# Attention sums: 448 accumulating exponentials on ScalarE in place of 512 products with ones on TensorE

## The chip, the cores and the metric

The kernel runs on one core of a Trainium2 chip. The metric is the device time of one execution in microseconds (us), lower is better; the number shown is the median of three runs. One further execution was taken by the hardware profiler, and all lines of the profile come from that one. The engines are named as the profile names them: PE is TensorE's matmuls, PEld its weight loads, DVE is VectorE, ACT is ScalarE, POOL is GpSimd, SP is SyncE.

## The reference

Sixteen sequences of 128 tokens, each token 128 wide, pass through four layers. Each layer adds two gated blocks to `x`: an attention to a context of the same shape, and a feed-forward block. Layers 0, 1 and 3 have mixtures of experts (8, 16 and 32 experts), layer 2 has a block of 64 slots. The change touches the attentions of layers 2 and 3, which have 16 heads of width 8:

```python
# layer 2
scores = jnp.einsum('bhqd,bhkd->bhqk', q, k) * scale
scores = jnp.where(mask == 0, jnp.float32(-1000000000.0), scores)
attn = jax.nn.softmax(scores, axis=-1)
out = jnp.einsum('bhqk,bhkd->bhqd', attn, v)
# layer 3: heads 0-7 at full length, heads 8-15 on every second token
for i, f in enumerate((1, 2)):
    hs = slice(i * HPS, (i + 1) * HPS)
    Qd, Kd, Vd = Q[:, hs, ::f], K[:, hs, ::f], V[:, hs, ::f]
    scores = jnp.einsum('bhqd,bhkd->bhqk', Qd, Kd) * inv_scale
    attn = jax.nn.softmax(scores, axis=-1)
    o = jnp.einsum('bhqk,bhkd->bhqd', attn, Vd)
    outs.append(_upsample_linear(o, S))
```

So for each query and head the kernel needs the largest score, the exponentials of the scores minus it, their sum over the keys, and the values weighted by exponential over sum.

## The kernel before

The sixteen sequences are worked in four groups of four (512 tokens). `experts()` is one long stream of expert steps over the layers 1 and 3 (and part of layer 0), a Python generator; between its steps the main program writes down the attentions of other groups. In the stretch of interest the order in the program is: attention 2 of group g when layer 1's experts of group g are done, attention 3 of group g when the slots of layer 2 for that group are done. The slots and the routing of the next expert block are written down between expert steps. Which instruction an engine runs when is laid down before the launch by the framework's scheduler: it takes what is ready, and what stands earlier in the program goes first. At run time each engine works through its own list in order and waits on semaphores. `in_turn` fixes the order of some matmuls among themselves. `nc.any` leaves it to the scheduler whether a copy runs on VectorE or ScalarE.

An expert step (`gated` and `down`) is two matmuls of 128x512 into the banks `pg` and `pu` (L445, L446), a tanh on ScalarE (L450), two products on VectorE (L451, L457), a product with the routing weight on GpSimd (L461), and, two steps later, the third matmul (L1036). Attentions take their PSUM banks from `ps_mm` (four banks of 512 numbers); the experts, the slots and the routings take theirs from `ps_x` (three banks) and `ps_acc` (one).

An attention tile covers 128 queries of eight or sixteen heads so that its scores fill four banks, four blocks of 128 in each. Attention 2 has four tiles a group, attention 3 two and a half one (the heads on every second token, two halves of 64 rows): 28 tiles in all, 24 full and 4 half. A tile goes so:

- First scores `ps`, queries on the partitions, keys along the row (L588 for the mask and L593 in attention 2, L739 and L772 in attention 3).
- `maxima`: VectorE takes the largest of each block, four instructions (L481), into columns of `mp`.
- `mp` is transposed on TensorE (L599, L745, L778) and added to the spare rows of `qT` (L600, L747, L779), so that the second product comes out with the maximum taken off.
- Second scores `ps`, keys on the partitions, queries along the row (L603 for the mask and L609, L754, L787). They need the same four banks.
- ScalarE takes the exponential of each bank into `pts` (L615, L760, L793), three buffers.
- `weighted` (L483): for each of the four banks four products of the values with `pts` into `po[:, 0, :]` (L487), and four products of `own` with `pts` into `po[:, 1, :]` (L490). `own` holds ones in the eight columns of a head, so the second gives the sum of the exponentials, repeated on the eight rows that hold this head's values. The half tile has eight and eight. `po` lies in a bank of `ps_mm` too (in the half tile in two).
- `over_weights` (L493): VectorE takes the reciprocal of the sums (L495) and multiplies (L496).

A matmul of 4-byte numbers shows as two records in the profile, a transpose as one.

Of the kernel before, what the change touches and what calls it, by code (L numbers as in the profile page):

```python
# [10 lines left out]
F32 = mybir.dt.float32  # L11
# [6 lines left out]
P = 128  # L18
# [8 lines left out]
DK = 8  # L27
# [32 lines left out]
def flamingo(ctx, tc, x_in, ctx_in, mask_in, w1, w2, w3, wslot, wsmall, slots, cols_in, rows_in, consts_in,  # L60
# [371 lines left out]
    def in_turn(chain, ins):  # L432

        if chain:
            tc.add_manual_dep(ins.ins, chain[-1].name,
                              mybir.DependencyInfo(mybir.DependencyClass.NoSync, mybir.DependencyReason.DATA),
                              reason="in_turn")
        chain[:] = [ins.ins]
# [35 lines left out]
    def value(rows, t, h):  # L474

        at = 24 + 32 * h - DK * (h % 4)
        return vp[rows, t, at:at + 32]

    def maxima(mp, i, src, n, k):

        nc.vector.tensor_reduce(mp[:, 0:n, 32 * i + 16:32 * i + 18], src, AX.X, ALU.max)  # L481

    def weighted(chain, heads, r, first, last):  # L483


        for po, jj, vcols, pts, rows in heads:
            in_turn(chain, nc.tensor.matmul(out=po[32 * jj:32 * jj + 32, 0, :], lhsT=vcols, rhs=pts, start=first, stop=last,  # L487
                                     skip_group_check=True))
        for po, jj, vcols, pts, rows in heads:
            in_turn(chain, nc.tensor.matmul(out=po[32 * jj:32 * jj + 32, 1, :], lhsT=own[rows, r, :], rhs=pts, start=False,  # L490
                                     stop=last, skip_group_check=True))

    def over_weights(o, po, n):  # L493
        rc = work.tile([P, P], F32, tag="rcw", name="rcw")
        nc.vector.reciprocal(rc[:, :n], po[:, 1, :])  # L495
        nc.vector.tensor_tensor(o, po[:, 0, :], rc[:, :n], ALU.mult)  # L496


# [69 lines left out]
    def attention_2(g):  # L568
# [15 lines left out]
        for t in range(GB):  # L584
# [5 lines left out]
            for s in range(2):  # L590
                for i in range(4):
                    rr = slice(32 * i, 32 * i + 32)
                    nc.tensor.matmul(out=split(ps[i])[:, 2 * s:2 * s + 2, :], lhsT=qT[rr, s, b], rhs=kTm[rr, s, :, b],  # L593
                                     start=False, stop=True, skip_group_check=True)
            for i in range(4):
                maxima(mp[:, 2 * t:2 * t + 2], i, ps[i][:].rearrange("p (s j k) -> p s j k", s=2, j=2), 2, P)
            pt = tr_tile()
            for s in range(2):
                nc.tensor.transpose(pt[:, s * P:(s + 1) * P], mp[:, 2 * t + s, :], ident[:])  # L599
# [13 lines left out]
            for i in range(4):  # L613
                pts = work.tile([P, 4, P], F32, tag="pts", name="pts", bufs=3)
                nc.scalar.activation(pts[:], split(ps[i]), AF.Exp, scale=scale8)  # L615
                weighted(chain, [(po, jj, value(slice(0, P), t, 4 * jj + i), pts[:, jj, :], slice(0, P)) for jj in range(4)],
                         i, i == 0, i == 3)
            over_weights(oT[:, b], po, P)
        py = split(mm_tile())
        for t in range(GB):  # L620
            mm(py[:, t, :], oT[:, t * P:(t + 1) * P], w(W2, 1))
# [83 lines left out]
    def attention_3(g):  # L705
# [27 lines left out]
        for p in range(2):  # L733
            ps = [mm_tile() for _ in range(4)]
            for u in range(2):
                b = slice((2 * p + u) * P, (2 * p + u + 1) * P)
                for i in range(4):
                    rr = slice(32 * i, 32 * i + 32)
                    nc.tensor.matmul(out=split(ps[i])[:, 2 * u:2 * u + 2, :], lhsT=qa[rr, b], rhs=ka[rr, :, b],  # L739
                                     start=True, stop=True)  # L740
            for i in range(4):
                maxima(mp[:, 2 * p:2 * p + 2], i, ps[i][:].rearrange("p (u j k) -> p u j k", u=2, j=2), 2, P)
            pt = tr_tile()
            for u in range(2):
                nc.tensor.transpose(pt[:, u * P:(u + 1) * P], mp[:, 2 * p + u, :], ident[:])  # L745
# [12 lines left out]
            for i in range(4):  # L758
                pts = work.tile([P, 4, P], F32, tag="pts", name="pts", bufs=3)
                nc.scalar.activation(pts[:], split(ps[i]), AF.Exp, scale=scale8)  # L760
                weighted(chain, [(po, jj, value(slice(0, P), 2 * p + jj // 2, 4 * (jj % 2) + i), pts[:, jj, :], slice(0, P))
                          for jj in range(4)], i, i == 0, i == 3)
            over_weights(oa[:, p, :], po, P)


        ps = [mm_tile()[:, 0:G2].rearrange("p (p2 j k) -> p p2 j k", p2=2, j=2) for _ in range(4)]
# [6 lines left out]
                                     start=True, stop=True)  # L773
        for i in range(4):
            maxima(mp[:, 4:6], i, ps[i], 2, HALF)
        pt = tr_tile()
        for p in range(2):
            nc.tensor.transpose(pt[:, p * P:(p + 1) * P], mp[:, 4 + p, :], ident[:])  # L778
# [12 lines left out]
        for i in range(4):  # L791
            pts = work.tile([P, 4, P], F32, tag="pts", name="pts", bufs=3)
            nc.scalar.activation(pts[:, :, 0:HALF], ps[i], AF.Exp, scale=scale8)  # L793
            halves = [slice(u * HALF, (u + 1) * HALF) for u in range(2)]
            weighted(chain, [(po[u], jj, value(halves[u], jj // 2, 8 + 4 * (jj % 2) + i), pts[halves[u], jj, 0:HALF], halves[u])
                      for jj in range(4) for u in range(2)], i, i == 0, i == 3)
        for u in range(2):
            over_weights(ob[:, u, :], po[u], HALF)


        pz = [mm_tile() for _ in range(2)]
# [352 lines left out]
    W3, W3H = load("w3", w3[:, 2 * D:3 * D]), weights_by_head("w3h", w3)  # L1154

    mp = blank("mp", [P, 8, P])
    own = blank("own", [P, 4, 32])
    for r in range(4):
        nc.gpsimd.memset(own[:, r, DK * r:DK * r + DK], 1.0)


    perm = work.tile([P, 2, P], F32, tag="pts", name="perm", bufs=3)
# [172 lines left out]
```

## Time and profile before

| | |
|---|---|
| median of 3 runs | 928.96 us (928.27 to 929.91) |
| profiled execution | 930.84 us, its span 929.1 us |
| mean granted clock of TensorE | 0.965 |
| busy: PE, PEld | 834.3 us (90%), 468.5 us (50%) |
| busy: DVE, ACT, POOL | 580.6 us (62%), 259.3 us (28%), 282.6 us (30%) |
| instructions: PE, DVE, ACT, POOL | 6183, 1628, 457, 283 |

The span runs from the first to the last instruction; what lies around it is 930.84 - 929.1 = 1.7 us. A busy share is a mean over stages with different limits. The profile's page ends its chain of waits with PE 54%, DVE 21%, POOL 8% and ACT 4% of the span. The costliest groups are GpSimd's products with routing weights (L461, 126 of 1278 ns, 161.0 us) and the three matmuls of the expert steps (L446, L1036 and L445, 288 records each, 154 to 156 us each). Of the attentions: the maxima L481 (65.8 us in 112 instructions), the products with values L487 and with ones L490, the exponentials L615 (64 of 602 ns, 33.6 us), and the reciprocals L495.

In a line of a group stand the line of the kernel, the engine, the operation, output and input with their shapes, the count, the busy time in us and the mean of one in ns, then the idle time of the engine ahead of them and what ended it. In a line of the timeline stand the start in us, the length in us, the engine, the line, the operation and how many were merged; in brackets the idle time before it and what ended that.

### The profile page before, as it was taken

The page shows a single profiled execution, that of the slowest core. Times are in us where ns is not written, and L with a number is a line of the kernel's source. Part 1 is how long each engine was busy: PE and PEld are TensorE (multiplying, and loading weights), DVE is VectorE, ACT ScalarE, POOL GpSimd, SP SyncE. Part 2 cuts the span into 40 slices and gives each one's busy share as a digit, 9 for nine tenths or more (in the row PEclk, how much of TensorE's full clock was granted, in tenths as well). Part 3 has the DMA queues.
Part 4 walks back from the last instruction along what each step waited for, and adds up shares of the span by engine and source line. Part 5 has one row for each costly group of instructions (what it writes and reads, how often), then busy time and mean ns, then how long its engine had stood idle before and what let it go on. Part 6 is the DMA issues. An engine that isn't in the chain of part 4 may idle for free.

```text
span 929.1 us, 16015 instructions
## 1 busy us (share of the span) xinstructions
PE 834.3 (90%) x6183; PEld 468.5 (50%) x6183; DVE 580.6 (62%) x1628; ACT 259.3 (28%) x457; POOL 282.6 (30%) x283
## 2 busy tenths in 40 slices
PE   3889399877999999999899999999989998999997
PEld 3554289534544554455455555555554554554443
DVE  4756252566977475666675866677666668566622
ACT  1222166221321222232223222223222232322321
POOL 3326521353233124311421113421114223313443
PEclk9979699978999999999999999999999999999999
DMA  9711212552121012100202112310002111211231
GB/s 305 211 17 40 64 46 79 159 162 63 24 69 44 27 35 80 46 21 28 69 35 67 35 47 62 123 37 24 24 24 72 35 48 46 76 51 49 94 103 34
DMA packets 55677, 62.12 MB, mean 67 GB/s; under 512 B 14312, under 2 KB 33512, under 8 KB 55472
## 3 DMA queue, kind: packets, MB, share of 16 engines
q1 hardware_dynamic: 53776, 55.90, 19.9%
q0 software_dynamic: 1536, 3.15, 1.1%
q10 hardware_dynamic: 288, 2.03, 0.6%
q8 instruction: 49, 0.80, 0.4%
q14 instruction: 28, 0.23, 0.1%
HBM read 53.97 MB, written 7.09 MB: 66 GB/s over the span
## 4 chain that ended last, share of the span: by engine, by line
PE 54%; DVE 21%; POOL 8%; issue 8%; ACT 4%; DMA 2%; another core or an unknown queue 1%; SPq 1%; POOLq 0%; DVEq 0%; ACTq 0%
PE mm L108 8%; PE acc L1036 7%; PE pg L445 7%; PE pu L446 7%; POOL hw L461 3%; DVE sg L451 3%; PE mm L593 2%; PE po L487 2%; DVE h L457 2%; DVE mp L481 2%; POOL rs L260 2%; POOL y L1017 2%; DVE xn L264 2%; PE tr L244 2%; PE po L490 2%
## 5 line engine op out<-in xcount | busy, mean ns | idle before, releaser
L461 POOL TENSOR_TENSOR hw<-h,cb 128x512 f32<-128x512 f32 x126 | 161.0, 1278 | 459.4 <-DVE h L457 348.1
L446 PE MATMUL pu<-xnTx,wall 128*128 128x512 f32 x288 | 156.4, 626 | 14.9 <-DVE sg L451 13.1
L1036 PE MATMUL acc<-hw,wall 128*128 128x512 f32 x288 | 153.9, 618 | 10.6 <-DVE h L457 9.9
L445 PE MATMUL pg<-xnTx,wall 128*128 128x512 f32 x288 | 154.8, 620 | 7.8 <-issue 4.7
L450 ACT ACTIVATE sg<-pg 128x512 f32<-128x512 f32 x123 | 73.6, 598 | 244.7 <-PE pg L445 230.5
L457 DVE TENSOR_TENSOR h<-sg,pu 128x512 f32<-128x512 f32 x145 | 99.1, 683 | 60.9 <-PE pu L446 40.7
L451 DVE SCALAR_TENSOR_TENSOR sg<-sg,pg 128x512 f32<-128x512 f32 x123 | 83.6, 680 | 51.4 <-ACT sg L450 51.3
L1036 PEld LDWEIGHTS acc<-hw,wall 128*128 128x128 f32 x288 | 55.1, 198 | 71.3 <-issue 53.0
L446 PEld LDWEIGHTS pu<-xnTx,wall 128*128 128x128 f32 x288 | 52.4, 197 | 75.9 <-issue 39.1
L481 DVE TENSOR_REDUCE mp<-mm 128x4 f32<-128x512 f32 (+1 forms) x112 | 65.8, 645 | 21.1 <-PE mm L593 19.9
L445 PEld LDWEIGHTS pg<-xnTx,wall 128*128 128x128 f32 x288 | 50.1, 194 | 50.2 <-issue 35.1
L495 DVE RECIPROCAL rcw<-po 128x128 f32<-128x128 f32 (+1 forms) x28 | 25.2, 900 | 57.1 <-PE po L490 44.8
L264 DVE TENSOR_SCALAR xn<-x,mv,rs 128x128 f32<-128x128 f32 x116 | 40.3, 399 | 25.4 <-POOL rs L260 25.4
L615 ACT ACTIVATE pts<-mm 128x512 f32<-128x512 f32 x64 | 33.6, 602 | 73.3 <-PE mm L609 73.3
L487 PE MATMUL po<-pts,vp 128*32 128x128 f32 (+1 forms) x896 | 46.1, 274 | 7.6 <-ACT pts L615 6.7
L260 POOL TENSOR_TENSOR rs<-ve,neghalf 128x4 f32<-128x4 f32 x32 | 33.2, 1037 | 61.8 <-DVE ve L258 61.7
L490 PE MATMUL po<-pts,own 128*32 128x128 f32 (+1 forms) x896 | 44.3, 266 | 0.5 <-issue 0.5
L453 ACT ACTIVATE sg<-pg 128x512 f32<-128x512 f32 x33 | 19.7, 597 | 67.9 <-PE pg L445 58.4
L487 PEld LDWEIGHTS po<-pts,vp 128*32 128x32 f32 (+1 forms) x896 | 21.3, 108 | 29.9 <-ACT pts L615 14.0
L254 DVE BATCH_NORM_STATS2 st<-x 128x6 f32<-128x128 f32 x128 | 29.5, 280 | 10.2 <-DMA x<-in_x 9.9
L593 PE MATMUL mm<-kTm,qT 32*128 32x256 f32 x256 | 30.5, 413 | 0.0
L1017 POOL DMA_INDIRECT y<-yd,to x24 | 23.7, 987 | 21.7 <-DMA yd<-yb 8.8
(335 smaller groups left out, 1226.0 us busy)
## 6 DMA issues: line engine op xcount, KB each, us to landing
cb<-combD SPq DMA_DIRECT2D x72, 256.0 KB
cb<-combD SPq DMA_DIRECT2D x128, 128.0 KB
wall<-in_gu SPq DMA_DIRECT2D x24, 256.0 KB
wall<-in_dn SPq DMA_DIRECT2D x12, 256.0 KB
xb<-xd SPq DMA_DIRECT2D x7, 256.0 KB
yd<-yb SPq DMA_DIRECT2D x7, 256.0 KB
xd<-vp ACTq DMA_DIRECT2D x1, 1072.0 KB
x<-in_x SPq DMA_DIRECT2D x4, 256.0 KB
```

What stands on the lines that cost most here:

```text
L108: nc.tensor.matmul(out=o, lhsT=l, rhs=r, start=start, stop=stop)
L264: nc.vector.tensor_scalar(xn[:, t, :], x[:, t, :], mv[:, t, 0:1], rs[:, t:t + 1], ALU.subtract, ALU.mult)
L445: in_turn(chain, nc.tensor.matmul(out=pg[:], lhsT=w[:, 0], rhs=xnT[:], start=True, stop=True))
L446: in_turn(chain, nc.tensor.matmul(out=pu[:], lhsT=w[:, 1], rhs=xnT[:], start=True, stop=True))
L450: nc.scalar.activation(sg[:], pg[:], AF.Tanh, scale=0.5)
L451: nc.vector.scalar_tensor_tensor(sg[:], sg[:], 1.0, pg[:], ALU.add, ALU.mult)
L457: nc.vector.tensor_tensor(h[:], sg[:], pu[:], ALU.mult)
L461: (nc.vector if vector else nc.gpsimd).tensor_tensor(hw[:], h[:], cb[:], ALU.mult)
L481: nc.vector.tensor_reduce(mp[:, 0:n, 32 * i + 16:32 * i + 18], src, AX.X, ALU.max)
L487: in_turn(chain, nc.tensor.matmul(out=po[32 * jj:32 * jj + 32, 0, :], lhsT=vcols, rhs=pts, start=first, stop=last, skip_group_check=True))
L490: in_turn(chain, nc.tensor.matmul(out=po[32 * jj:32 * jj + 32, 1, :], lhsT=own[rows, r, :], rhs=pts, start=False, stop=last, skip_group_ch ...
L1036: in_turn(chain, nc.tensor.matmul(out=acc[0][:], lhsT=w[:, 2], rhs=h[:], start=n == 0, stop=last))
```

## The change

The sums are no longer formed by products. A new function `sums_of_weights` follows the maxima of the first scores. For each of the four banks VectorE scales the maxima (`top`), and ScalarE takes the exponential of each block of the first scores in place, with the block's scaled maximum as bias and with the sum over the row as a second output (`accum_out`) into a column of `sums`. VectorE takes the reciprocals of 16 columns, GpSimd spreads each over eight columns (`over`). At the end of the tile `over_sums` turns `over` to the layout of the values by one product with the identity, copies that out of PSUM, and multiplies. The products with `own`, the tile `own` and its five fills go.

```diff
-    def weighted(chain, heads, r, first, last):
+    def sums_of_weights(mp, ps, k):
+        sums = small.tile([P, 16], F32, tag="sums", name="sums")
+        for i in range(4):
+            top = small.tile([P, 2, 2], F32, tag="mxs", name="mxs", bufs=4)
+            nc.vector.tensor_scalar(top[:], mp[:, :, 32 * i + 16:32 * i + 18], -scale8, None, ALU.mult)
+            for a in range(2):
+                for j in range(2):
+                    at = 8 * a + 4 * j + i
+                    nc.scalar.activation(ps[i][:, a, j, :], ps[i][:, a, j, :], AF.Exp, bias=top[:, a, j:j + 1], scale=scale8,
+                                         accum_out=sums[:, at:at + 1])
+        nc.vector.reciprocal(sums[:], sums[:])
+        over = small.tile([P, 16, DK], F32, tag="over", name="over")
+        nc.gpsimd.tensor_copy(over[:], bc(sums[:], 2, DK))
+        return over[:].rearrange("p h d -> p (h d)")
+
+    def weighted(chain, heads, first, last):
...
-        for po, jj, vcols, pts, rows in heads:
-            in_turn(chain, nc.tensor.matmul(out=po[32 * jj:32 * jj + 32, 1, :], lhsT=own[rows, r, :], rhs=pts, start=False,
-                                     stop=last, skip_group_check=True))
-
-    def over_weights(o, po, n):
+    def over_sums(chain, o, po, over, rows):
+        n = o.shape[1]
+        in_turn(chain, nc.tensor.matmul(out=po[:, 1, :], lhsT=over[rows, :], rhs=ident[rows, rows], start=False,
+                                        stop=True, skip_group_check=True))
         rc = work.tile([P, P], F32, tag="rcw", name="rcw")
-        nc.vector.reciprocal(rc[:, :n], po[:, 1, :])
+        nc.any.tensor_copy(rc[:, :n], po[:, 1, :])
         nc.vector.tensor_tensor(o, po[:, 0, :], rc[:, :n], ALU.mult)
...
             for i in range(4):
-                maxima(mp[:, 2 * t:2 * t + 2], i, ps[i][:].rearrange("p (s j k) -> p s j k", s=2, j=2), 2, P)
+                maxima(mp[:, 2 * t:2 * t + 2], i, ps[i], 2, P)
+            over = sums_of_weights(mp[:, 2 * t:2 * t + 2], ps, P)
             pt = tr_tile()
...
-            over_weights(oT[:, b], po, P)
+            over_sums(chain, oT[:, b], po, over, slice(0, P))
...
-    own = blank("own", [P, 4, 32])
-    for r in range(4):
-        nc.gpsimd.memset(own[:, r, DK * r:DK * r + DK], 1.0)
```

The same three edits (the call behind the maxima, the shorter `weighted`, `over_sums` at the end) stand in the full tiles of attention 3 and in its half tile, where `over_sums` is called for each of the two halves.

## The prediction

> **What bounds the kernel now.** I read the forty slices of the span first, then the attention stretches by window, then one attention tile in order of time, then the groups by line and shape.
>
> ```profile
> PE   3889399877999999999899999999989998999997
> ACT  1222166221321222232223222223222232322321
> PEclk9979699978999999999999999999999999999999
> ```
>
> From slice 12 on (attention 2 starts at 282 us) TensorE is busy nine tenths at the full granted clock, and ScalarE two to three tenths. In the eight attention stretches (282-340, 374-440, 475-510, 510-560, 600-635, 635-690, 720-760 and 808-850 us, together 381 us) TensorE is busy 361 us, VectorE 253, ScalarE 105. So a matmul taken away looks like a gain, and ScalarE looks free. One tile of attention 2 shows what the averages hide:
>
> ```profile
> 295.36 2.48 DVE L481 TENSOR_REDUCE mp<-mm 128x4 f32<-128x512 f32 x4
> ...
> 299.15 1.17 PE L609 MATMUL mm<-qT,kTm 32*128 32x128 f32 x32
> ...
> 300.40 1.57 ACT L615 ACTIVATE pts<-mm 128x512 f32<-128x512 f32 x3 [5.68 <-PE mm L609]
> ...
> 303.72 0.96 DVE L495 RECIPROCAL rcw<-po 128x128 f32<-128x128 f32 x1 [0.53 <-PE po L490]
> ...
> 305.06 0.39 PE L588 MATMUL mm<-mb,identb 128*128 128x512 bf16 x1
> ...
> 306.14 2.49 DVE L481 TENSOR_REDUCE mp<-mm 128x4 f32<-128x512 f32 x4 [1.14 <-PE mm L593]
> ```
>
> This is a closed chain: four maxima, their transposes, the mask product L603, the second scores L609, four exponentials L615, the sums of values, a reciprocal, a product, and only then the next tile's last first-pass bank (305.06). From maxima to maxima it is 10.78 us, and the second tile repeats it at 10.80. The four matmul banks are all taken by the first scores, then by the second, and `po` is one of the four; no two tiles overlap. TensorE is busy 10.18 us of it only because one expert step (pg, pu and acc, some 3.3 us) fills the chain's holes. The two limits are balanced: shorten TensorE's work and the chain stays; lengthen the chain and only more expert steps can pay for it. The end follows the chain too: attention 3 of the last group ends at 846 us, its routing turns into the last experts' first step near 876, and 17 steps follow to 929.
>
> **What it removes on TensorE.**
>
> ```profile
> L490 PE MATMUL po<-pts,own 128*32 128x128 f32 x768 | 38.6, 273 | 0.0
> ...
> L490 PEld LDWEIGHTS po<-pts,own 128*32 128x32 f32 x768 | 23.0, 110 | 0.0
> ```
>
> With the two 64-row forms (5.8 us each) the ones-products are 38.6 + 11.6 = 50.2 us of matmul rows. I don't take 50. Perfetto Trace Analysis ("Identifying the Most-Contended Engine") in the Trainium skill says that matmul busy time is a bad measure and weight-load time a better one; that is 23.0 + 3.7 + 3.6 = 30.3 us. The timeline decides below both: at 301.55, 301.77, 301.99, 302.20 and 302.42 us the groups of eight records, values and ones in turn, start 0.22 us apart, though each reads 0.40 long. Four groups of ones are 0.9 us a tile, 24 full tiles and 4 half ones about 24 us. The added product with the identity (two records; the transposes L599 are the nearest row, 0.21 us of busy time each) takes 0.3 us with its gap, 28 tiles about 9 us. **TensorE's net: 0.6 us a tile, some 15 us of the kernel**. By the matmul rows it would be 50 - 9 = 41 us, 1.5 a tile, and the sum at the end 22 us lower; by the rule's loads 21 us, and the sum 4 lower.
>
> **What it adds on ScalarE.** 16 exponentials of 128x128 in each full tile, 128x64 in each half one: 448 instructions, where 457 ran in all before. No row has an accumulator output. The nearest:
>
> ```profile
> L615 ACT ACTIVATE pts<-mm 128x512 f32<-128x512 f32 x64 | 33.6, 602 | 73.3 <-PE mm L609 73.3
> ...
> L793 ACT ACTIVATE pts<-mm 128x256 f32<-128x256 f32 x16 | 5.3, 384 | 7.9 <-PE mm L787 5.3 <-PE mm L490 2.6
> ...
> L719 ACT ACTIVATE qT<-mm,hcols 128x256 f32<-128x256 f32 x4 | 1.9, 466 | 0.0
> ...
> L807 ACT COPY z<-mm 128x128 f32<-128x128 f32 x2 | 0.4, 268 | 0.7 <-PE mm L108 0.7
> ```
>
> A 128x128 read from PSUM is 0.27 us. A bias that is a tile's column adds 0.08 (466 against 384), so 0.35; three L615 in a row take 1.57 us, 0.08 less each than alone, so 0.27 in a run. That is the lower end. For the accumulator: the ScalarE page of the Trainium skill (ScalarE: Activation LUTs, "What it computes") names the output without a price; VectorE: DVE Perf Modes ("Two Vector instructions with no wait between them") says that on VectorE such an operation is two instructions, the second an accumulator read. That rule speaks against this change. No run here shows it for ScalarE. If it holds, the overlap goes and a short read is added: 0.602 and 0.384 us give a fixed part of 0.166 for an instruction with no elements; upper end 0.35 + 0.17 = 0.52. I take 0.44, an overlapped read of 0.09 behind an exponential that no longer overlaps. By the row alone a tile's 16 are 4.3 us, and the sum at the end would be 914 us; by the rule 7.0 and 975; at the most 8.3. Over the kernel ScalarE goes from 259 to about 455 us, not a bound by itself.
>
> **The wait this makes.** It was "L603 waits for maxima"; it becomes "L603 and L609 (L754 in attention 3) wait for the sixteen exponentials", because these work in place in the four banks that the second scores need. Maxima to L609 took 299.15 - 295.36 = 3.8 us. After: the exponentials can start 0.9 us after the first maxima began (one maximum, one 0.19 us scaling as L258) or, as the four maxima stand first in the program, at 2.8; I take 2.3. Then 7.0 of exponentials, 0.3 for the last bank's mask product: 9.6. Plus 5.8. Back at the tile's end, the 0.96 us reciprocal gives way to the product (0.3) and a copy from PSUM (0.27 to 0.29 by L807, on either engine): minus 0.4, and minus 0.1 of fewer products. **A full tile's chain grows by 5.3 us.** In the half tile maxima to L787 was 3.4 us (498.46 to 501.89); 1.5 + 16 x 0.39 + 0.3 - 3.4 - 0.5 = plus 4.1. Sum: 24 x 5.3 + 4 x 4.1 = 144 us.
>
> Behind the sixteen on ScalarE's queue stand the experts' `sg` (L450), the copies of transposes and the slots' Gelu; VectorE's L451 and TensorE's next pg wait for `sg`. The experts have three banks of their own, so about one step's matmuls run during a burst and then stop.
>
> **What is paid back.** Expert steps drawn into the longer tiles leave the stretches between the attentions (340-374, 440-475, 560-600, 690-720, 760-808: 187 us). I count 3.3 us a tile for one more step, and the freed 0.6: 3.9 us, for the 25 tiles before the last group's attention 3 = 98 us. The last three tiles draw from 850-884, which the last routing takes anyway, so they pay back nothing.
>
> **Edits at no cost.** VectorE: 112 scalings at 0.19 us add 21 us, 32 reciprocals (23.0 + about 4 us) become 28 of 0.17: about even, at 62% busy; not covered, the four scalings would delay each tile 0.8 us (the 2.8 above has one). GpSimd's spread of `over` (below 0.6 us, L982 copies 128x512 in 0.61) lies beside the second scores, 4 us before its reader; late, it delays the closing product and the next tile's bank. The blank `own` and its four fills fall on GpSimd before attention 2. Exp and Tanh alternate today without table loads, so none is added.
>
> **Sum.** 144 - 98 = plus 46 us. The profiled execution was 930.84 us (span 929.1), 1.9 above the median of the three runs: 930.8 + 46 - 1.9, **975 us**.
>
> **Rivals.**
> Forecast, the chain grows and is paid back in part: 932 to 1000, chance 0.50.
> *TensorE stays the bound, faster.* The cover is ample: the stretches between hold 48 expert steps, and ScalarE is three quarters idle. With 0.27 us an exponential the tile grows 2.6 us, 24 x 2.6 + 4 x 1.4 = 68, less than one step pays back; then TensorE's 15 us decide: **914 us**. It turns at the price where 24x + 4(x - 1.2) = 98, x = 3.7 us a tile, 0.34 us an exponential. Against it: the accumulator must be read somehow. Chance 0.20.
> *The dear exponential.* 0.52 us and a start at 2.8: 2.8 + 8.3 + 0.3 - 3.8 - 0.5 = 7.1 us a tile, 24 x 7.1 + 4 x 5.6 = 193 - 98 = plus 95: **1024 us**. Chance 0.18.
> *The burst starves the experts:* `sg` stands behind it, no further step is drawn in, only 0.6 x 25 = 15 returns: 144 - 15 = plus 129, **1058 us**. Against it: three expert banks and spare steps. Chance 0.08.
> Within 0.2%, about what a measurement of this kernel can tell from no change: 0.04, where growth and payback cancel.
> So faster 0.20, same 0.04, slower 0.76. The range, 905 to 1022, takes in most of the faster case and nearly all of the dear one; the likeliest case alone is 932 to 1000.
>
> **What would show it.** The ones-products gone; 448 exponentials with bias, with or without a row of their own for the accumulator; maxima to maxima near 16 us instead of 10.8; TensorE's L603 and L754 waiting on ScalarE; ScalarE at about 450 us; two expert steps a tile and shorter stretches between; TensorE's share down to about 84%. An exponential below 0.34 us, or tiles that still follow each other within 14 us, would prove me wrong, and so would a scheduled order that puts many more expert steps into the burst.

## The result and the profile after

The changed kernel takes **1046.91 us** (median of five runs, 1046.49 to 1054.15) against 928.96: the ratio is 1.1286 [1.1248, 1.1324]. The forecast of 975 us and its range, 905 to 1022, both lie below it. The profiled execution is the longest of the five (span 1052.5 us); all sums below are made against the span of before, 929.1 us, so they have **123 us** to explain. One execution of experiment 4 and one of experiment 12 fell into a slower state and are left out of their medians below (with them 1010.98 and 1068.89 us).

From the forty slices of the page after:

```profile
PE   4987699779999999799988889988789988998997
...
ACT  1222454223255427433546342654442561254221
...
PEclk9979799899999999989898589899579889978999
```

ScalarE has risen from two or three tenths to mostly four to six where the attentions are. TensorE has eight, not nine, and its clock row, which stood at 9 from slice 11 on, now dips, twice to 5. The mean granted clock fell from 0.965 to 0.902. The costs by line and shape, ScalarE first, from the groups:

```profile
L493 ACT ACTIVATE mm<-mm,mxs 128x128 f32<-128x128 f32 x384 | 133.2, 372 | 85.9 <-DVE mxs L489 77.9 <-PE pu L446 7.3
L493 ACT ACTIVATION_READ_ACCUMULATOR mm<-mm,mxs 128x1 f32 x448 | 106.9, 239 | 0.0
```

The accumulator has an instruction of its own, behind every exponential. In the tile it is seen how much of it overlaps (timeline of the first tile of attention 2, after):

```profile
294.91 2.48 DVE L481 TENSOR_REDUCE mp<-mm 128x4 f32<-128x512 f32 x4
...
297.55 0.34 ACT L493 ACTIVATE mm<-mm,mxs 128x128 f32<-128x128 f32 x1 [3.28 <-DVE mxs L489]
...
297.82 0.19 ACT L493 ACTIVATION_READ_ACCUMULATOR mm<-mm,mxs 128x1 f32 x1
297.91 0.33 ACT L493 ACTIVATE mm<-mm,mxs 128x128 f32<-128x128 f32 x1
...
303.06 1.17 ACT L450 ACTIVATE sg<-pg 128x512 f32<-128x512 f32 x2
...
303.61 1.16 PE L629 MATMUL mm<-qT,kTm 32*128 32x128 f32 x22
...
304.67 2.23 ACT L635 ACTIVATE pts<-mm 128x512 f32<-128x512 f32 x4 [0.44 <-PE mm L629]
...
309.91 2.48 DVE L481 TENSOR_REDUCE mp<-mm 128x4 f32<-128x512 f32 x4 [1.46 <-PE mm L611]
```

Sixteen pairs fill 297.55 to 303.06, 0.34 us a pair. Two tanh of the experts have waited behind them (303.06). The last second scores start 8.7 us after the maxima, where it was 3.8, and the next maxima come after 15.0 us instead of 10.8. In this tile it is the picture that was forecast, down to the two expert steps; in other stretches, as shown below, it is not.

**A ledger of the 123 us.** The first maximum marks the start of each tile. Seven stretches of three or four tiles contain 18 whole distances from tile to tile; they became 97.6 us longer, 5.4 each. Each of the seven gaps between stretches also contains one tile; at 5.4 us (an estimate, since three of the seven are half tiles) this hides 38 us of growth in them. The last stretch, from its first tile to the end, grew 16.6 us. Growth in all: 152 us. The gaps themselves grew only 9.6 us, so without their hidden tiles they shrank 28 us: that is the payback. Against the forecast:

| | growth a tile | growth | paid back | sum |
|---|---|---|---|---|
| forecast | 5.3 (half tile 4.1) | 144 | 98 | +46 |
| measured, after | 5.4 | 152 | 28 | +123 |

Growth came near. **The payback is the term that failed**: little more than a quarter of it came.

**The steps that were not drawn in.** The forecast wanted one expert step more in each tile. Each step has one tanh, so the tanh instructions in a stretch count its steps. In the 18 distances there are 19 before and 25 after: 6 more, where 18 more had been counted on. In the first two stretches, attention 2 of groups 0 and 1, they came (5 before, 12 after, in 6 distances); in attention 2 of groups 2 and 3 there are fewer than before. One of these stretches, before, then after (tanh L450; columns: window, its length, busy time with instructions of ACT, granted clock, DMA share, GB/s):

```profile
520.13:555.95 35.82, 2.41 (x4) 1.00 0.15 46
551.53:605.61 54.08, 1.31 (x2) 0.72 0.10 25
```

**Where the expert steps stood still.** After 563.07 us the next tanh of the expert stream starts at 614.34. In the 51 us between, no tanh of an expert step runs, and the same stop comes again at 726.9; before, the longest such stop in these stages was 18 us. Windows of that stop, after (columns: window, its length, then busy time with instructions of PE, PEld, DVE, ACT and POOL, granted clock, DMA share, GB/s):

```profile
563.00:580.00 17.00, 12.60 (x90) 6.64 (x84) 8.93 (x45) 8.23 (x38) 2.38 (x4) 0.78 0.14 32
580.00:590.00 10.00, 9.01 (x64) 4.65 (x62) 1.95 (x4) 1.46 (x3) 0.00 (x0) 0.50 0.00 0
590.00:614.00 24.00, 16.46 (x110) 9.38 (x111) 7.30 (x22) 13.73 (x69) 0.29 (x1) 0.64 0.00 1
```

In the middle TensorE looks busy, 9.01 of 10 us, but it has 64 matmul records and a clock of 0.50: little work at half speed. GpSimd and the DMA queues, which serve the experts, stand at zero. What ends the stop is in the chain that ended last (start, length, what):

```profile
605.63 2.46 DVE mp L481 x4
608.09 0.29 DVE mxs L489 x4
608.38 0.33 DVE sum L365
...
608.95 0.44 DVE combs L373
```

`sum` (L365) and `combs` (L373) are the routing of layer 2's slots. Its input is old:

```profile
539.37 0.97 DVE L380 TENSOR_TENSOR sme<-sme,sel 128x256 f32<-128x256 f32 x1
...
608.29 0.41 DVE L365 TENSOR_REDUCE sum<-sme 128x4 f32<-128x256 f32 x1
...
608.95 0.43 DVE L373 TENSOR_TENSOR combs<-sme,rsum 128x256 f32<-128x256 f32 x1
```

The slots' exponentials are multiplied at 539.37, and summed 69 us later. Before, in the same group, the two stood 0.45 us apart:

```profile
526.73 0.42 DVE L380 TENSOR_TENSOR sme<-sme,sel 128x256 f32<-128x256 f32 x1
527.18 0.42 DVE L365 TENSOR_REDUCE sum<-sme 128x4 f32<-128x256 f32 x1
```

The reason is a name. `sums_of_weights` takes its tile with `tag="sums"`; the slots' routing takes its `sum` with `tag_of("sum")`, which appends the side's letter "s", and so is "sums" as well. Both use the same ring of two buffers, handed out in the order of the program, and the slots' sum has to wait until the attention tiles written down ahead of it have let go of theirs. The slots feed the next layer's routing, and the experts wait for that. Nothing in the diff shows it unless one puts the other names beside it.

### The profile page after: what moved, and what is told of

Same layout as the page of the kernel before. It is cut to its first block, busy times and chain, and to the rows that moved or that the text cites. A ratio compares the mean times of both kernels' runs of the same rounds, so it can differ in the third digit from the quotient of the medians.

```text
span 1052.5 us, 15204 instructions
## 1 busy us (share of the span) xinstructions
PE 917.7 (87%) x5223; PEld 508.1 (48%) x5223; DVE 574.6 (55%) x1736; ACT 420.6 (40%) x1385; POOL 289.2 (27%) x306
## 4 chain that ended last, share of the span: by engine, by line
PE 51%; DVE 19%; ACT 12%; issue 7%; POOL 7%; DMA 3%; SPq 0%; POOLq 0%; DVEq 0%; ACTq 0%
ACT mm L493 9%; PE pg L445 8%; PE mm L108 7%; PE pu L446 7%; PE acc L1058 6%; DVE mp L481 5%; POOL hw L461 3%; PE po L504 3%; DVE sg L451 2%; PE mm L629 2%; PE mm L611 2%; POOL rs L260 2%; PE tr L244 2%; DVE h L457 2%; PE mm L758 1%
## 5 line engine op out<-in xcount | busy, mean ns | idle before, releaser
L493 ACT ACTIVATE mm<-mm,mxs 128x128 f32<-128x128 f32 (+1 forms) x448 | 152.0, 365 | 97.1 <-DVE mxs L489 89.2
L446 PE MATMUL pu<-xnTx,wall 128*128 128x512 f32 x288 | 161.7, 645 | 15.2 <-DVE sg L451 11.1
L445 PE MATMUL pg<-xnTx,wall 128*128 128x512 f32 x288 | 163.6, 652 | 9.8 <-DVE h L457 4.9
L1058 PE MATMUL acc<-hw,wall 128*128 128x512 f32 x288 | 156.8, 629 | 0.7 <-POOL hw L461 0.7
L450 ACT ACTIVATE sg<-pg 128x512 f32<-128x512 f32 x123 | 74.0, 611 | 180.0 <-PE pg L445 177.8
L493 ACT ACTIVATION_READ_ACCUMULATOR mm<-mm,mxs 128x1 f32 x448 | 106.9, 239 | 0.0
L445 PEld LDWEIGHTS pg<-xnTx,wall 128*128 128x128 f32 x288 | 53.4, 205 | 58.0 <-issue 36.7
L497 POOL COPY over<-sums 128x128 f32<-128x128 f32 x28 | 8.2, 293 | 218.0 <-DVE sums L495 218.0
L629 PEld LDWEIGHTS mm<-qT,kTm 32*128 32x128 f32 x512 | 34.2, 219 | 22.3 <-issue 22.3
L629 PE MATMUL mm<-qT,kTm 32*128 32x128 f32 x512 | 42.9, 330 | 0.0
```

What stands on the lines that cost most here:

```text
L445: in_turn(chain, nc.tensor.matmul(out=pg[:], lhsT=w[:, 0], rhs=xnT[:], start=True, stop=True))
L446: in_turn(chain, nc.tensor.matmul(out=pu[:], lhsT=w[:, 1], rhs=xnT[:], start=True, stop=True))
L450: nc.scalar.activation(sg[:], pg[:], AF.Tanh, scale=0.5)
L493: nc.scalar.activation(ps[i][:, a, j, :], ps[i][:, a, j, :], AF.Exp, bias=top[:, a, j:j + 1], scale=scale8, accum_out=sums[:, at:at + 1])
L629: nc.tensor.matmul(out=split(ps[i])[:, 2 * s + j, :], lhsT=kTm[rr, s, j, b], rhs=qT[rr, s, b], start=False, stop=True, skip_group_check=True)
L1058: in_turn(chain, nc.tensor.matmul(out=acc[0][:], lhsT=w[:, 2], rhs=h[:], start=n == 0, stop=last))
```

## Experiments

All times are medians; ratios are against the kernel before, on the same chip. Its median was 928.4 to 931.2 us from chip to chip, and each form is scheduled anew, so a few us between two forms decide nothing. The ledgers (made as above, in us against the span of before) stand at the end of this section.

**1. A ring of its own.** The change with one word changed.

```diff
-        sums = small.tile([P, 16], F32, tag="sums", name="sums")
+        sums = small.tile([P, 16], F32, tag="wsums", name="sums")
```

> The changed kernel with one word changed: the attention's sums lie in a ring of buffers of their own, not in the ring named sums, which the slots' softmax (over_sum on side s) uses too. Theory R (shared ring): buffers of one ring are given out in program order, so the slots' sum waits for the last attention tile written before it; 23 to 70 us pass between the slots' exponential and its sum in the trace, behind it the experts stop for about 50 us twice, TensorE idles and its granted clock falls. Then this run has that distance at some 3 us as before, no stop of the experts over 20 us, a granted clock of 0.95 or more, and 940 to 970 us. Theory B (the burst of exponentials holds the four banks and alone makes the loss): 1035 to 1050 us, clock near 0.90.

1004.26 us, ratio 1.0798 [1.073, 1.0867]: between the two theories. The shared ring costs 43 of the 118 us between the medians, the rest is something else. VectorE's timeline shows the tie gone:

```profile
537.17 0.81 DVE L380 TENSOR_TENSOR sme<-sme,sel 128x256 f32<-128x256 f32 x1
...
538.50 0.41 DVE L365 TENSOR_REDUCE sum<-sme 128x4 f32<-128x256 f32 x1
...
539.63 1.50 DVE L373 TENSOR_TENSOR combs<-sme,rsum 128x256 f32<-128x256 f32 x1
```

The same windows as above now have the full clock, and GpSimd works in both:

```profile
563.00:580.00 17.00, 15.62 (x128) 8.45 (x129) 11.65 (x39) 8.50 (x38) 2.83 (x3) 1.00 0.15 50
580.00:590.00 10.00, 9.72 (x50) 4.63 (x47) 4.76 (x12) 6.41 (x32) 1.26 (x1) 1.00 0.26 76
```

The stretch that held 2 tanh now holds 5:

```profile
550.21:597.73 47.52, 3.28 (x5) 1.00 0.16 51
```

So does the same stretch of the next group, and all five other stretches keep their counts: 31 in all, 12 more than before. The ring alone had kept 6 steps out. The ledger: growth 136 us, payback 62. All later forms of the change have a ring of their own.

**2. The tie alone.** The kernel before, with one tile an attention tile taken from the ring "sums", filled by a scaling and read by a small copy.

```diff
+    def one_more(mp):
+        sums = small.tile([P, 16], F32, tag="sums", name="sums")
+        nc.vector.tensor_scalar(sums[:], mp[:, 0, 16:32], -scale8, None, ALU.mult)
+        over = small.tile([P, 16], F32, tag="over", name="over")
+        nc.gpsimd.tensor_copy(over[:], sums[:])
...
+            one_more(mp[:, 2 * t:2 * t + 2])
```

> The kernel before, its ones-products kept, with one tile a attention tile more in the ring named sums (one scaling of 128x16 on VectorE, one copy on GpSimd, 28 of each, their results used nowhere). Theory R: the slots' sum waits here too, though no exponential was added: 955 to 1010 us, a granted clock below 0.96. Theory B: nothing but 28 x 0.2 us on VectorE: 929 to 936 us.

933.42 us, ratio 1.0044 [1.0025, 1.0063]: the theory that expected 955 us or more failed. The tie is there, and the slots' sum comes 32 us behind its input:

```profile
525.12 0.42 DVE L380 TENSOR_TENSOR sme<-sme,sel 128x256 f32<-128x256 f32 x1
...
557.08 0.41 DVE L365 TENSOR_REDUCE sum<-sme 128x4 f32<-128x256 f32 x1
```

Yet it costs 4 to 5 us at the most, the added instructions included. The tie is dear only together with the burst. That it grows with the length of the tiles (32 us here, 69 in the changed kernel) is seen; how a late sum turns into 43 us was not tested.

**3. All but the burst.** Experiment 1 without the 448 exponentials; the sums are set to one, so the output is not normalised by the weights.

```diff
-        for i in range(4):
...
-                    nc.scalar.activation(ps[i][:, a, j, :], ps[i][:, a, j, :], AF.Exp, bias=top[:, a, j:j + 1], scale=scale8,
-                                         accum_out=sums[:, at:at + 1])
+        nc.vector.tensor_scalar(sums[:], mp[:, 0, 0:16], 0.0, 1.0, ALU.mult, ALU.add)
```

> As e1_own_ring, but without the 448 exponentials and their scalings: the sums are set to one, so the output is not normalised. It leaves what the change saves. If TensorE's time counts: 24 us of ones-products less 9 of the closing products, 900 to 920 us. If the closed chain of a tile decides, only the reciprocal's 0.4 us a tile go: 915 to 930 us. Both theories have the same for this run; e1 less e3 is the price of the burst: 15 to 60 us by theory R, over 110 by theory B.

925.24 us, ratio 0.9951 [0.9932, 0.997]. So little, some 4 us, is what the removed products bring with the other edits in place (the 112 scalings are gone too). The burst with its scalings costs 1004.26 - 925.24 = **79 us**. With the 43 of the ring and less the 4, this makes up the whole 118.

**4. Bank by bank.** Experiment 1 with maximum, scaling and exponentials of one bank written down before those of the next, so that the burst can start after one maximum.

```diff
         for i in range(4):
+            maxima(mp, i, ps[i], 2, k)
...
-            for i in range(4):
-                maxima(mp[:, 2 * t:2 * t + 2], i, ps[i], 2, P)
```

> As e1_own_ring, but maxima, scaling and exponentials written down bank by bank, so that the first exponential can follow the first maximum (0.9 us after it began) and not the fourth (2.6 us). If the tile's chain through the banks sets the end: 1.7 us a tile, 15 to 40 us below e1_own_ring. If the expert steps fill the chain anyway: within 5 us of it.

1010.32 us, ratio 1.0845 [1.0768, 1.0923]. A miss, since nothing is won: a tile grows 3.8 us instead of 4.9, but only 22 us are paid back instead of 62, and only 23 tanh stand in the 18 distances. A shorter tile alone is not worth its length.

**5. Half the burst.** Eight exponentials a tile, the other eight sums set to one (so half the heads are not normalised).

```diff
-        for i in range(4):
+        nc.gpsimd.memset(sums[:], 1.0)
+        for i in range(2):
```

> As e1_own_ring, with the exponentials and scalings of the first two banks alone (8 a tile, not 16); the other eight sums are set to one, so half of the heads are not normalised. e1_own_ring took 1004 us, without a burst 925. If each exponential delays the tile's chain by its own length: half of the 79 us, 958 to 972 us. If a burst under some 3 us lies beside the expert steps: 925 to 945 us. If the number doesn't matter, only that ScalarE comes between the two score passes: 985 to 1005 us.

953.31 us, ratio 1.027 [1.0219, 1.032]. Eight cost 28 us over experiment 3, sixteen cost 79: the first half is cheap, the second dear, and the time lies between the first two theories.

**6 and 11. More work for TensorE.** Experiment 1 with 6, then with 14 products of the mask in each full tile, which nothing reads.

```diff
...
+            for _ in range(6):
+                nc.tensor.matmul(out=pt[:, 2 * P:4 * P], lhsT=identb[:], rhs=bc(mb[:], 1, 2), start=True, stop=True)
...
```

> As e1_own_ring, with six matmuls of bf16 128x256 more in each full tile, behind the maxima's addition to qT, into the unused half of the transposes' bank, their result read by nothing: about 1.2 us of work in the time in which TensorE waits for the exponentials. If the lower granted clock (0.938 over the span of e1_own_ring) comes from TensorE's waits and costs time by itself: clock 0.955 or more and 985 to 1000 us, faster with more work. If the clock is a symptom only: 1004 to 1030 us.

> The form with a ring of its own (1004 us), with 14 bf16 products a full tile that nothing reads, instead of the 6 that made it 994 us. At the 0.27 us of a row with 6 they are 192 x 0.27 = 52 us of further TensorE time. Theory C (part of the burst's price is the clock that TensorE loses while it waits; more work keeps more of it): no slower than with 6, 980 to 995 us, granted clock over 0.95. Rival W (6 took what there was to take; the rest is ScalarE's time): 1000 to 1045 us, at a clock over 0.95 all the same.

With 6: 994.29 us, ratio 1.0698 [1.066, 1.0736]. With 14: 1000.96 us, ratio 1.0773 [1.0722, 1.0825]. The granted clock, as the mean of four executions each, is 0.938 in experiment 1, 0.952 with 6 and 0.946 with 14. The groups of the second, by form:

```profile
L622 PE MATMUL tr<-mb,identb 128*128 128x256 bf16 x224 | 27.0, 272 | 1.5 <-DVE qT L620 1.5
...
L772 PE MATMUL tr<-mb,identb 128*128 128x256 bf16 x112 | 13.5, 273 | 0.0
```

The 336 records overlap; they take 40.5 us of TensorE, and the kernel is no slower for them. So **TensorE's amount of work is not what bounds the changed kernel**: 40 us put into the hole beside the burst cost nothing. That more work brings back clock is seen. That it brings back time is likely for 6 (all its four executions are faster than those of 1, and the intervals just overlap), not shown for 14; a different order of instructions is not ruled out. The figure written down ahead for the eight further products (52 us) came from single lengths; by the groups they are 21.

**7. A shorter end of the tile, before.** The kernel before, where one copy takes the place of reciprocal and product (not normalised).

```diff
-        nc.vector.reciprocal(rc[:, :n], po[:, 1, :])
-        nc.vector.tensor_tensor(o, po[:, 0, :], rc[:, :n], ALU.mult)
+        nc.vector.tensor_copy(o, po[:, 0, :])
```

> The kernel before with the reciprocal and the product at a tile's end replaced by one copy of the values' sums: the output is not normalised, the ones-products stay. It takes 0.9 us of VectorE from the end of each tile's chain and leaves TensorE its work. If the chain of a tile sets its length: 24 x 0.9 + 8 x 0.5 = some 26 us at the most, 903 to 918 us. If TensorE sets it: 924 to 930 us.

919.66 us, ratio 0.9892 [0.9851, 0.9933], between the two theories. Some 0.9 us a tile, 26 us over 28 tiles, brought 10. The end of the tile's chain does set time in the kernel before, but at less than half of its length.

**8 and 10. The burst off the banks, normalised later.** ScalarE copies the scores to SBUF (four copies a tile), the burst works there, and a group is normalised when its tiles are done. In 10 the burst is also held behind its own tile's `pts`.

```diff
...
+            sc = kept(ps, P)
...
-            over_sums(chain, oT[:, b], po, over, slice(0, P))
+            raw(oT[:, b], po)
+            overs.append((sums_of_weights(mp[:, 2 * t:2 * t + 2], sc, P), slice(0, P)))
+        over_sums(oT[:], overs, P)
```

> As e1_own_ring, but ScalarE copies the first scores to SBUF (four copies of 128x512 a tile) and takes the 16 exponentials there after the second pass's; the values' sums are copied out of PSUM unnormalised, and each group's division comes once, after its tiles. ScalarE has 28 x 2.1 us more to do, but the four banks are held by the copies alone, 2.1 us and not 5.4. If the hold on the banks is the burst's price: 935 to 970 us. If it is ScalarE's time, the experts' tanh behind the burst: 1000 us or more.

> The form that keeps the scores in SBUF (994 us), with the 16 small exponentials of a tile held behind the last pts of the same tile on ScalarE. Theory Q (it was their place in ScalarE's queue, ahead of pts, that made the tile long): 950 to 970 us. Rival S (ScalarE's own time in the attention tiles, wherever it stands: the exponentials then stand ahead of the next tile's copies and the experts' tanh): 985 to 1005 us.

8: 994.02 us, ratio 1.0721 [1.0664, 1.0777]. 10: 986.97 us, ratio 1.0609 [1.0561, 1.0657]. In 8 the second scores start 4.0 us after the maxima again, as before the change, and then wait for a `pts` that stands behind the burst on ScalarE:

```profile
396.61 0.40 ACT L502 ACTIVATE kept<-kept,mxs 128x128 f32<-128x128 f32 x1
396.90 0.20 ACT L502 ACTIVATION_READ_ACCUMULATOR kept<-kept,mxs 128x1 f32 x1
397.00 1.55 ACT L646 ACTIVATE pts<-mm 128x512 f32<-128x512 f32 x3
```

In 10 that place in the queue is gone and a tile grows by 0.8 us only, yet 7 us are all that is won, as the rival S expected, and the gaps become 20 us longer instead of shorter. Both forms carry the copies, some 55 us more of ScalarE, so they do not yet tell banks from queue.

**12 to 15. Banks, queue or ScalarE's time.** Four forms in which the burst reads a constant in SBUF and writes SBUF, so that it holds no bank and needs no copies. In 12 and 14 it stands at its old place ahead of `pts`, and its (other) sums go to the closing product. In 13 and 15 it is held behind `pts`, and nobody reads its sums (they are set to one as in 3). None of the four is normalised by the weights. In 12 and 13 all exponentials write one tile, in 14 and 15 two by turns. The line of 14:

```diff
-                    nc.scalar.activation(ps[i][:, a, j, :], ps[i][:, a, j, :], AF.Exp, bias=top[:, a, j:j + 1], scale=scale8,
+                    nc.scalar.activation(seen[:, j, 0:k], ident[:, 0:k], AF.Exp, bias=top[:, a, j:j + 1], scale=scale8,
```

> The form with a ring of its own (1004 us), whose 16 small exponentials a tile stand where they stood but read and write SBUF instead of the four banks of the scores (sums of other numbers, so the output is not normalised by the weights). Nothing of the burst holds a bank; pts still queue behind it on ScalarE, and the closing product still waits for it. Theory K (the banks held until the burst ends are most of its price): 935 to 960 us. Theory S (ScalarE's time between the maxima and pts is most of it): 980 to 1000 us.

> The form without the burst (925 us; sums set to one, not normalised), with 16 small exponentials a tile on SBUF, held behind the last pts of their tile, whose sums nobody reads: ScalarE's time alone, with no bank, no pts and no product behind it but the experts' tanh and the next tile's pts. Theory T (the time itself is the price, since tanh steps wait for it): 950 to 975 us. Theory Q (only what stands in front of the burst's own tile counts): 925 to 940 us.

12: 1064.53 us, ratio 1.146 [1.1366, 1.1555], above both theories. 13: 961.01 us, ratio 1.0318 [1.0267, 1.0368], where theory T expected it. The timeline of 13 shows what was wrong with the pair: one output tile makes each exponential start 0.53 us after the one before.

```profile
561.02 0.40 ACT L502 ACTIVATE seen<-ident,mxs 128x128 f32<-128x128 f32 x1
561.33 0.19 ACT L502 ACTIVATION_READ_ACCUMULATOR seen<-ident,mxs 128x1 f32 x1
561.55 0.40 ACT L502 ACTIVATE seen<-ident,mxs 128x128 f32<-128x128 f32 x1
```

> The off-bank burst, at its place before pts, with two output tiles by turns (one output tile for all made each exponential wait for the one before: 0.53 us apart, not 0.34; again the output is not normalised by the weights). At 0.39 us apart, the pace of the form that kept the scores in SBUF, a burst of 16 shrinks from 8.5 to 6.2 us, against 5.4 in the banks. Theory L (ScalarE's length of the burst makes the price, banks or not): 1005 to 1030 us. Theory K (the banks are most of the price and 1069 us was the slow pace): 940 to 975 us.

> The burst held behind its tile's pts, unread (961 us), with two output tiles by turns, so that 16 take 6.2 us, not 8.5 (sums set to one, not normalised). Theory L (ScalarE's length, even off every chain, is paid in tanh steps that wait): 940 to 955 us. Rival M (off the chain the length doesn't matter as such): 958 to 964 us as before.

With two output tiles the pace is 0.38 us (timeline of 15):

```profile
563.21 0.39 ACT L502 ACTIVATE seen<-ident,mxs 128x128 f32<-128x128 f32 x1
563.50 0.19 ACT L502 ACTIVATION_READ_ACCUMULATOR seen<-ident,mxs 128x1 f32 x1
563.59 0.39 ACT L502 ACTIVATE seen<-ident,mxs 128x128 f32<-128x128 f32 x1
```

14: 1008.75 us, ratio 1.0856 [1.0806, 1.0906]. 15: 964.66 us, ratio 1.0367 [1.0316, 1.0417]. Three readings. **The banks are not most of the price**: without holding them (14) the kernel is as slow as with them (1004.26). The burst in 14 is some 0.6 us longer (0.38 against 0.34 us apart). At the price of the slow pace, 56 us for the 2.1 us by which the burst of 12 is longer than that of 14, this is some 15 us, so by this estimate the banks may still cost about 10. TensorE then waits for `pts` instead, from 14's waits (line, what it waits for, us, times, longest):

```profile
PE po L505 <- ACT pts L636: 25.6, 15, 2.6
PE po L505 <- ACT pts L782: 13.8, 9, 2.2
```

**The place ahead of `pts`, with the product that needs the sums, is 44 us** (14 against 15). **A burst behind `pts`, whose sums nobody reads, still costs 36 to 39 us** (13 and 15 against 3). The two add up to the 84 us between 14 and 3, against 79 for the burst in its banks. The second part is not ScalarE's time alone. The scalings are back (112 on VectorE, which 3 does not have), and they wait for the exponentials of the tile before, which still read the ring `mxs` of four buffers; from 15's waits, and 19.2 us in 13:

```profile
DVE mxs L498 <- ACT seen L502: 5.3, 11, 1.1
```

And the tiles of 15 are 1.0 us longer, where those of 3 are 0.2, so the burst is not off every tile's chain. A form with the scalings and without exponentials would have to part the two. Ahead of `pts` the length of the burst counts steeply (0.53 against 0.38 us: 56 us); behind `pts` it was not seen to count at all (961 and 965).

**9. The end of the tile, without the change.** What experiment 7 hinted at, in a form that computes the same as before: both halves of `po` are copied out of the bank first, and normalised in SBUF.

```diff
-        rc = work.tile([P, P], F32, tag="rcw", name="rcw")
-        nc.vector.reciprocal(rc[:, :n], po[:, 1, :])
-        nc.vector.tensor_tensor(o, po[:, 0, :], rc[:, :n], ALU.mult)
+        rc = work.tile([P, 2, P], F32, tag="rcw", name="rcw")
+        nc.any.tensor_copy(rc[:, :, :n], po)
+        nc.vector.reciprocal(rc[:, 1, :n], rc[:, 1, :n])
+        nc.vector.tensor_tensor(o, rc[:, 0, :n], rc[:, 1, :n], ALU.mult)
```

> The kernel before, with both halves of po copied out of their bank by one instruction, and the reciprocal and the product then made from SBUF. Theory A (the reciprocal, 0.96 us, and the product hold the bank of the closed chain, and no reader waits soon for oT): most of what leaving the reciprocal out brought, 921 to 926 us. Rival B (VectorE's longer queue, or the copy's own place behind the exponentials, gives it back): 928 to 934 us.

**919.06 us, ratio 0.9878 [0.9838, 0.9918]: 1.2% faster than the kernel before**, as much as experiment 7 brought and more than theory A expected. Its groups by form:

```profile
L496 DVE RECIPROCAL rcw<-rcw 128x128 f32<-128x128 f32 x24 | 22.9, 952 | 52.3 <-ACT rcw L495 52.3
...
L495 ACT COPY rcw<-po 128x256 f32<-128x256 f32 x24 | 8.9, 372 | 17.9 <-PE po L490 17.9
```

The bank is let go after a copy of 0.37 us on ScalarE, and the reciprocal, still 0.95 us on VectorE, can lie beside the next tile.

**The ledgers.**

| kernel | a tile | growth | paid back | tanh in the 18 distances | ScalarE busy |
|---|---|---|---|---|---|
| before | | | | 19 | 259 us |
| after | +5.4 | 152 | 28 | 25 | 421 |
| 1, own ring | +4.9 | 136 | 62 | 31 | 418 |
| 3, no burst | +0.2 | 5 | 11 | 17 | 267 |
| 4, bank by bank | +3.8 | 104 | 22 | 23 | 421 |
| 6 and 11, more TensorE work | +5.2, +5.1 | 144, 141 | 75, 72 | 31, 31 | 418, 419 |
| 8, off the banks | +2.5 | 73 | 10 | 21 | 479 |
| 10, 8 behind `pts` | +0.8 | 35 | -20 | 23 | 473 |
| 14, off the banks, no copies | +3.8 | 104 | 28 | 27 | 429 |
| 15, behind `pts`, unread | +1.0 | 29 | -1 | 18 | 419 |

Growth less payback is the difference of the spans, but for the start of the first tile, which moved by up to 5 us. From 1 to 4 and from 8 to 10 the tiles grow some 30 to 40 us less, and nearly as much or more is lost in the gaps. Of the forms with the whole burst in the banks and a ring of their own (1, 4, 6 and 11), those that draw in 31 steps are paid back 62 to 75 us, the one that draws in 23 only 22.

**The clock's part.** From 282 us to the end TensorE was busy 606.6 of 647 us before (clock 0.99), 687.9 of 770 after (0.89), 660.0 of 719 in experiment 1 (0.94), 601.1 of 640 in 3 (0.99) and 620.1 of 681 in 15 (0.97): 81 and 53 us longer in the changed kernel and in 1, with fewer instructions. In the changed kernel some of its falls stand at holes that the burst makes (timeline):

```profile
573.56 0.69 PE L619 MATMUL tr<-ident,mp 128*128 128x128 f32 x2 [3.58 <-ACT mm L493]
```

TensorE stood still for 3.58 us until an exponential had let a bank go; the 2 us windows from 574 on have a clock of 0.50. The Trainium skill (TensorE: Matmul & The Clock Gate, "HAM oscillation — how this bites in real kernels") gives as its rule that there be no idle gap of more than about 3.4 us, and this agrees. But in experiment 1 the clock falls in a tile without such a hole. Its second scores at 499.82 had waited 1.23 us for the burst, the longest wait of TensorE in the 25 us before; then, in windows of 2 us:

```profile
498.00:500.00 2.00, 0.77 (x17) 0.58 (x12) 1.27 (x5) 1.94 (x8) 0.77 (x2) 1.00 0.32 104
500.00:502.00 2.00, 1.88 (x29) 1.29 (x29) 1.23 (x3) 1.45 (x4) 2.00 (x3) 1.00 0.04 8
502.00:504.00 2.00, 2.00 (x20) 1.10 (x19) 0.00 (x0) 0.38 (x1) 0.66 (x1) 0.56 0.09 25
504.00:506.00 2.00, 2.00 (x14) 1.52 (x14) 0.29 (x1) 0.27 (x1) 0.00 (x0) 0.50 0.40 107
```

and 0.50 until 512. The rule alone does not foresee this fall, and the measurement decides; which part the short wait has in it and which the thin work around it (TensorE busy 0.77 of 2 us) was not tested. An upper bound for what the clock costs, as an estimate: the missing share of the clock times the stretch, 0.06 x 719 = 43 us in experiment 1 and 0.11 x 770 = 85 in the changed kernel, against 0.01 x 647 = 6 before. It is a bound, since a slow TensorE that would have waited anyway costs nothing.

## Why the prediction failed

By its own steps:

- **Payback, 98 us. This step failed.** The prediction had 3.9 us for each of 25 tiles, since two expert steps instead of one would be drawn into each. They were not: in the 18 distances that can be counted, 6 further steps were drawn in instead of 18, and 28 us were paid back. Half of this is shown: with a ring of its own for the new tile there are 12 further steps and 62 us of payback, so the shared ring, which the prediction put at nothing by not naming it, took 33 us, and made tiles and end some 16 us longer. Of the 36 us that are still missing, 6 steps that did not come would be some 27 (an estimate: a third of 25 tiles at the prediction's 3.3 us). Why they did not come stays open. The runs show that it isn't TensorE's amount of work (in 6 and 11 the steps stay 31), nor for the most part the banks (14), and that a burst that nobody reads draws in no step at all (18 in 15) and still costs 36 to 39 us, so its time on ScalarE, "not a bound by itself" at 455 us, was not free. How this divides between late tanh instructions, VectorE's scalings and the clock (a bound of 0.03 x 681 = 20 us in 15) was not settled.
- **"The burst starves the experts", 1058 us at a chance of 0.08,** came near the time for another reason. It had `sg` behind the burst and no step drawn in. A third of the steps was drawn in; the experts starved where the slots' routing waited for a ring.
- **Growth, 144 us: near,** 152 in the changed kernel and 136 with a ring of its own, but in part by luck. Two of its terms were off. The exponential was set at 0.44 us and is 0.34: the accumulator's read is an instruction of its own, as the Trainium skill's rule for VectorE (VectorE: DVE Perf Modes, "Two Vector instructions with no wait between them") made likely, and this trace shows it for ScalarE, but the overlap did not go with it. This makes 1.6 us a tile less. The start of the burst, set at 2.3 us, was 2.64, and the clock put some of it back: the tile at 568.28 took 19.9 us, where it took 15.4 with a ring of its own at the full clock.
- **The faster rival's turning point, 0.34 us an exponential, was wrong.** That price came, and the kernel was 13% slower (8% with a ring of its own), since the point was worked out with the whole payback.
- **TensorE's saving, 15 us:** 4 in experiment 3. The matmul rows (41) and the weight loads (21) were the worse guesses, as argued, but 15 also counted, as it seems, what hung on a chain that TensorE did not set.
- **The clock** was taken as full throughout. It is not an input: where the experts stood still it was 0.50 to 0.78, and it may hold up to 85 of the 123 us.
- **Edits at no cost.** No instruction of TensorE waits for GpSimd's spread, and there are 16 table loads before and after. VectorE's four scalings stand ahead of the burst (0.29 us together at 608.09). The ring behind the new tile's name was not looked at, and it cost 43 us.

## What to carry to other kernels

A new tile's tag belongs to the cost of an edit: look up who else can have that ring, composed names too. Payback is worth only the steps that are in fact drawn into the longer stretch: count them, stretch by stretch, and follow what they wait for, not only the room on the engine that looks full. When a closed chain is found in the profile, look for what sits at its end only because it reads a bank: a copy of 0.37 us a tile was worth some 11 us.

## What the runs showed of the hardware

- An activation with an accumulator output is two instructions on ScalarE: one of 372 ns and a read of 239 ns in the mean at 128x128, which overlap to 0.34 us a pair in place in PSUM, and to 0.38 from SBUF.
- Successive activations with accumulator into one SBUF tile stand 0.53 us apart, into two by turns 0.38 (128x128, experiments 12 to 15). In the burst ahead of `pts` that was 56 us of the kernel.
- In experiment 1 TensorE's clock fell to half for some 10 us after a wait of no more than 1.23 us and thin work; added products that nobody reads raised the kernel's mean from 0.938 to 0.952 (6 a tile) and 0.946 (14).
